# A transformer block with 64 routed experts on one core: the last block of queries split in two, its last tile's rows stored apart, and the jobs put in another order

## The chip, the core and the metric

The kernel runs on one core of a Trainium2 chip, in one launch. The metric is the device time of one execution in microseconds (us). The core has five engines that run on their own instruction streams and wait for each other on semaphores: PE (matrix multiply, with its weight loads listed as PEld), DVE (vector), ACT (activation), POOL (GpSimd) and SP, which here only issues DMAs. DMAs that move whole tiles are issued from SP's queue; those that scatter rows by an index held in a tile are issued from POOL's.

## The reference: what is computed

Two sequences of 512 tokens, 256 features, 16 heads of 16; then 64 experts with inner width 96, 8 of them for each token. All is f32.

```python
x = _layernorm(x + attention(x))            # causal, with a bias per head that grows with the key's position
logits = x @ gate_w.T                       # 1024 tokens, 64 experts
probs = softmax(logits)
topk_w, topk_idx = top_k(probs, 8)          # weights made to sum to 1
g = einsum('th,ehi->tei', x, w1)
u = einsum('th,ehi->tei', x, w3)
y = einsum('te,tei,eih->th', combine_w, silu(g) * u, w2)
x = _layernorm(x + y)
```

The kernel computes each expert only for the tokens that chose it.

## The kernel before

Tokens are handled in 8 tiles of 128 (four per sequence). The attention goes through four blocks of two query tiles each, `blocks_ = [(0, 0), (0, 1), (1, 1), (1, 0)]` (sequence, half): a "short" block has the first two tiles of a sequence, and so one part of keys, a "long" block the last two and two parts. A block takes 8 steps, one for each pair of heads. In one step of the loop written out by hand (it fixes the order on PE, DVE and ACT), PE makes scores for pair `step` (`scores`, line 318; DVE takes maxima, line 324), and for pair `step - 3` the exponentials (`exponentials`: PE line 369, ACT line 379, and POOL cuts the triangle off with an affine select, line 384). Every second step, `values` multiplies with the values (line 406) and copies the result to `raw` (line 415).

When a block's last `values` is done, seven jobs are put into the following steps by `at`: `normalize`, `turn_context`, `project`, `norm` with `turn_x1`, `route`, `weigh` and `find_places`. Together they finish the attention's output, its layer norm, and the routing of two tiles: `find_places` counts with matmuls how many earlier tokens chose each expert (`seen` holds the counts so far) and gets for each token and choice a row number `to` (line 580). Then `dispatch` issues 8 scatters a tile on POOL's queue (line 587): each sends 128 rows of `x1` (the token, its weights, its places) into the DRAM buffer `xg`. There every expert has 288 rows: 128 first places, 32 more, and two further half blocks of 64. All of them are filled at the start with blank rows by 13 DMAs from SP (lines 194 and 195), 23,770 KB in all. POOL's stream keeps affine selects and scatters in a fixed order (`in_order`).

After the attention, a list stage on DVE (lines 697 to 787) works out from the counts which half blocks beyond the first 160 places are used. It needs two small index tiles from POOL (`number`, line 714, and `quarter`, line 752). Then comes a fallback loop (line 899) with a trip count read from the tile `extra` by every engine: it would treat all experts in full if the half blocks did not suffice. For these inputs its count is zero, but all engines meet there.

The expert stage has 88 jobs: 64 "one" (an expert's first 128 places), 16 "four" (the next 32 places of four experts together), 8 "pair" (two half blocks, found at run time). A job is fetched from `xg` by SP (line 793), turned by PE (line 799) and copied by DVE (line 801), multiplied (lines 810, 825, 834), and its 128 result rows are scattered into `results` in DRAM on POOL's queue (line 849). Jobs are fetched eight ahead in program order, and run through four steps, one after the other. A fetch waits for all 64 scatters (`after_scatters`). The weights of the first 18 experts are loaded at the start (`first_places`), 20 more into `room` during the attention (`load_then`), 8 more into `lates` behind it (these three go by pairs of experts), and the last 18 into `first_places` again as those come free. At the end, `results` is loaded back (line 995), eight rows a token are summed with `x1`, and the second layer norm goes out (lines 990 and 991).

## Time and profile before

| what | us |
|---|---|
| median of 9 runs (lowest and highest) | 463.23 (460.69 to 469.13) |
| the profiled execution: its time | 463.45 |
| the profiled execution: its span | 461.8 |
| span up to the last copy of `raw` (line 415) | about 205.6 |
| from there to the first scatter of the last block | about 26.3 |
| from that scatter to the first copy of a job's rows (line 801) | 28.2 |
| first to last scatter of results (line 849) | 266.8 to 426.3 |
| loading `results`, sums, second layer norm | about 33 |

The span runs from the first to the last instruction on the core; the time of the same execution is 1.65 us longer. Busy times: PE 360.1 us (78%), DVE 233.8, POOL 200.9, ACT 162.4. PE's busy time is modelled and overlaps itself, so it is not a bound by itself; the profile's row of the granted PE clock (10 tenths is full speed) tells how fast PE was allowed to go. "Idle before" an instruction is put down to the engine whose signal ended it.

### The profile page before, as it was taken

Reading aid. Unit: us, or ns where it says so; the run is one execution under the profiler, and the core shown is the slowest. Engines: PE = TensorE matmul, PEld = TensorE weight load, DVE = VectorE, ACT = ScalarE, POOL = GpSimd, SP = SyncE. Lnnn points to the kernel's source line nnn. Section 1 sums busy time; section 2 is a strip of 40 time slices with the busy share of each in tenths; the row PEclk is TensorE's granted clock in tenths of the full one; section 3 lists DMA queues with packets and bytes.
Section 4 is the critical chain, followed back from the end, with each engine's and each line's share of the span. In section 5 each row is a group of like instructions: output and inputs, shape, how many; then the busy total and the mean of one; then the engine's idle time right before and its main releaser. Section 6 shows DMA issues by size and latency. Waiting matters only on the chain. (4 is left out here: it accounts for less than half of the span.)

```text
span 461.8 us, 8458 instructions
## 1 busy us (share of the span) xinstructions
PE 360.1 (78%) x2546; PEld 237.2 (51%) x2546; DVE 233.8 (51%) x1040; ACT 162.4 (35%) x453; POOL 200.9 (43%) x278
## 2 busy tenths in 40 slices
PE   4499999998998899685300497898998898997493
PEld 2135545655664566453300365566665666765372
DVE  0744356764865256241390355455555565653185
ACT  2012423464446224424110144343434444435032
POOL 8911221211355337647477055354555455656000
PEclk9799999997999559656555599899999899999598
DMA  8999999999921202324833589997787757211793
GB/s 258 390 340 312 281 300 301 307 293 290 395 99 58 83 29 90 110 73 152 304 116 132 147 235 333 297 298 223 212 252 224 209 152 219 69 68 57 307 411 112
DMA packets 56591, 98.58 MB, mean 213 GB/s; under 512 B 7241, under 2 KB 40600, under 8 KB 55520
## 3 DMA queue, kind: packets, MB, share of 16 engines
q1 hardware_dynamic: 47728, 76.93, 53.8%
q0 software_dynamic: 7456, 19.46, 11.7%
q10 hardware_dynamic: 1360, 1.64, 1.1%
q8 instruction: 21, 0.34, 0.3%
q14 instruction: 26, 0.21, 0.1%
HBM read 52.38 MB, written 48.75 MB: 219 GB/s over the span
## 5 line engine op out<-in xcount | busy, mean ns | idle before, releaser
L849 POOL DMA_INDIRECT results<-y,rows x88 | 86.6, 984 | 87.6 <-DVE xT L801 27.6
L324 DVE CUSTOM_DVE_ANT_0 neg<-ps,mask 128x256 f32<-128x256 f32 (+3 forms) x128 | 57.5, 488 | 43.4 <-PE ps L318 37.1
L587 POOL DMA_INDIRECT xg<-x,to x64 | 63.5, 992 | 22.3 <-issue 16.7
L384 POOL TENSOR_SCALAR_AFFINE_SELECT pr<-pr 128x256 f32<-128x256 f32 x64 | 25.0, 408 | 109.8 <-ACT pr L379 109.8
L379 ACT ACTIVATE pr<-pt 128x384 f32<-128x384 f32 (+1 forms) x96 | 45.4, 523 | 48.4 <-PE pt L369 34.6
L799 PE MATMUL pxT<-ident,xb 128*128 128x128 f32 x176 | 36.4, 289 | 29.7 <-SPq L941 29.2
L801 DVE COPY xT<-pxT 128x256 f32<-128x256 f32 x88 | 37.2, 422 | 36.5 <-DMA xb<-xg 17.3
L799 PEld LDWEIGHTS pxT<-ident,xb 128*128 128x128 f32 x176 | 23.1, 145 | 47.4 <-issue 39.4
L818 ACT ACTIVATE s<-pg 128x96 f32<-128x96 f32 x88 | 22.2, 252 | 65.2 <-PE pg L810 29.4
L842 ACT COPY y<-py 128x256 f32<-128x256 f32 x88 | 32.9, 374 | 21.2 <-PE pxT L799 4.6
L810 PE MATMUL pg<-w,xT 128*32 128x192 f32 (+1 forms) x288 | 40.2, 348 | 0.2 <-DVE xT L801 0.2
L825 PE MATMUL paT<-ident,a 128*96 128x128 f32 x88 | 26.1, 297 | 14.5 <-DVE a L820 6.8
L369 PE MATMUL pt<-ql,kT 32*128 32x256 f32 (+1 forms) x192 | 33.5, 433 | 1.0 <-ACT pr L379 0.9
L273 PE MATMUL pq<-room 128*128 128x512 f32 x64 | 34.2, 671 | 0.0
L318 PE MATMUL ps<-room 32*128 32x128 f32 (+3 forms) x128 | 26.7, 492 | 6.4 <-DVE room L279 6.4
L318 PE MATMUL ps<-kT,qT 32*128 32x384 f32 (+3 forms) x128 | 31.5, 535 | 0.3 <-issue 0.2
L878 DVE CAST rows<-row 128x1 int32<-128x1 f32 x88 | 13.5, 154 | 34.0 <-DMA results<-y,rows 27.7
L810 PEld LDWEIGHTS pg<-w,xT 128*32 128x32 f32 (+1 forms) x288 | 27.9, 156 | 3.1 <-issue 0.8
L834 PE MATMUL py<-w,aT 96*32 96x256 f32 (+1 forms) x144 | 28.5, 390 | 0.0
L369 PE MATMUL pt<-ql,room 32*128 32x256 f32 (+1 forms) x192 | 27.0, 381 | 0.6 <-ACT pr L379 0.6
L827 ACT COPY aT<-paT 96x128 f32<-96x128 f32 x88 | 22.9, 260 | 12.2 <-PE paT L825 8.7
L369 PEld LDWEIGHTS pt<-ql,kT 32*128 32x128 f32 x192 | 22.9, 223 | 7.1 <-ACT pr L379 3.1
(200 smaller groups left out, 617.0 us busy)
## 6 DMA issues: line engine op xcount, KB each, us to landing
xg<-blank SPq DMA_DIRECT2D x8, 2632.0 KB
w<-in_wall_dram SPq DMA_DIRECT2D x18, 640.0 KB
xb<-xg SPq DMA_DIRECT2D x64, 164.5 KB
room<-in_wall_dram SPq DMA_DIRECT2D x10, 640.0 KB
room<-results SPq DMA_DIRECT2D x6, 1024.0 KB
wo<-in_wall_dram SPq DMA_DIRECT2D x16, 320.0 KB
xg<-blank SPq DMA_DIRECT2D x4, 658.0 KB
xb<-xg SPq DMA_DIRECT2D x64, 41.1 KB
```

Of the source, the lines that this page charges most:

```text
L273: nc.tensor.matmul(pq, lhsT=wqk_s[:, t, c, g * P : (g + 1) * P], rhs=xTs_[b][:, c, :], start=(c == 0), stop=(c == DC - 1))
L318: nc.tensor.matmul(ps[:, :n], lhsT=qT[b][r, g, q * P : (q + 1) * P], rhs=kT[b][r, g, :n], start=True, stop=True)
L324: nc.vector.tensor_tensor_reduce(out=junk[:, :n], in0=ps[:, :n], in1=mask[:, S - n :], scale=-1.0, scalar=BIG, op0=ALU.add, op1=ALU.min, a ...
L369: nc.tensor.matmul(pts[n][:, col : col + W2 - first], lhsT=kT[b][r, g, k * P : (k + 1) * P], rhs=ql[r, first:], start=True, stop=True,)
L379: nc.scalar.activation(pr[:, :cols], pts[n][:, :cols], AF.Exp, scale=SCALE)
L587: sc = nc.gpsimd.indirect_dma_start(out=xg[:, :], out_offset=bass.IndirectOffsetOnAxis(ap=tos[s][:, a, k : k + 1], axis=0), in_=x1[:, i + ...
L799: nc.tensor.transpose(pt[:, c * P : (c + 1) * P], xb[:, c * P : (c + 1) * P], ident)
L801: nc.vector.tensor_copy(xT, pt)
L810: nc.tensor.matmul(pg[r * m : (r + 1) * m, :], lhsT=xT[:, c * P + r * m : c * P + (r + 1) * m], rhs=w[:, c * 2 * I : (c + 1) * 2 * I], sta ...
L834: nc.tensor.matmul(py[r * m : (r + 1) * m, :], lhsT=aT[:I, r * m : (r + 1) * m], rhs=w[:I, DC * 2 * I :], start=True, stop=True,)
L842: nc.scalar.copy(y, py)
L849: a = nc.gpsimd.indirect_dma_start(out=results[:, :], out_offset=bass.IndirectOffsetOnAxis(ap=rows, axis=0), in_=y, in_offset=None, bounds ...
```

## The change

It has five parts.

- **Order and units of the attention.** Blocks become `(sequence, first tile, number of tiles)`; the second sequence's short block goes third, its long one last. The jobs behind a block now run per "unit": three units of two tiles, and the last block as two units of one tile each, both in the same steps. The jobs can stand in the middle of a step too, by a table of half steps for each block, and scatters are spread by a second table.
- **The last tile's rows apart.** For the very last unit, `find_places` takes the larger of the count so far and 128 as its base, so that its rows never fall among an expert's first 128 places. `seen` is then the count of used places, holes among them, and the separate count by a matmul goes.
- **Fetches that wait for less.** A "one" job waits for the first 56 scatters only; "four" and "pair" wait for all 64.
- **Order of the jobs.** Twenty "one" jobs go first, then each "four" with 2 or 3 "one" jobs, and a "pair" at every second "four". The late weights are asked for behind "four" jobs.
- **The fallback loop** moves from ahead of the jobs to behind them. The zeros that the loop wrote into `results` are now written always, by eight DMAs from SP of 1024 KB each during attention steps 16 to 23; before, these DMAs stood in the loop and never ran.

```diff
+    def no_results(i):
+        nc.sync.dma_start(
+            results[i * P * TOPK : (i + 1) * P * TOPK, :].rearrange("(p k) d -> p k d", k=TOPK),
+            blank[:, :D].unsqueeze(1).to_broadcast([P, TOPK, D]),
+        )
...
-        blocks_ = [(0, 0), (0, 1), (1, 1), (1, 0)]
+        blocks_ = [(0, 0, 2), (0, 2, 2), (1, 0, 2), (1, 2, 2)]
+        units = [(s, 0, 2) for s in range(len(blocks_) - 1)] + [(len(blocks_) - 1, a, 1) for a in range(2)]
...
+            else:
+                pm = room_for(s, 3)
+                nc.tensor.matmul(pm[:, 0, :], lhsT=ones, rhs=seen, start=True, stop=True)
+                nc.tensor.matmul(pm[:, 1, :], lhsT=before, rhs=mk[:, 0, :], start=True, stop=True)
+                nc.tensor.matmul(pm[:, 2, :], lhsT=ones, rhs=mk[:, 0, :], start=True, stop=True)
+                nc.vector.tensor_scalar(seen, pm[:, 0, :], float(P), None, ALU.max)
+                nc.vector.tensor_tensor(mine, pm[:, 1:2, :], seen.unsqueeze(1), ALU.add)
+                nc.vector.tensor_tensor(seen, pm[:, 2, :], seen, ALU.add)
...
-                scatters.append(sc)
+                if s == len(units) - 1:
+                    tc.add_to_no_dep_group("last scatters", sc.ins)
+                    last_scatters.append(sc)
+                else:
+                    scatters.append(sc)
                 in_order(sc, many=True)
...
+        HALF_STEPS = [[0, 1, 2, 4, 5, 6], [0, 2, 4, 7, 10, 12], [0, 1, 2, 4, 5, 6], [0, 2, 4, 6, 8, 10]]
+        SCATTER = [lambda k: k // 2, lambda k: k // 2, lambda k: k // 2, lambda k: 0]
...
+            for m in range(NT):
+                at(16 + m, no_results, m)
...
+                        for w in mine:
+                            nt = units[w][2]
+                            todo_ = [
+                                [(normalize, w, a) for a in range(nt)],
+                                [(turn_context, w)],
+                                [(project, w)],
+                                [(norm, w), (turn_x1, w)],
+                                [(route, w)],
+                                [(find_places, w), (weigh, w)],
+                            ]
+                            when = HALF_STEPS[s]
+                            for h, job in zip(when, todo_):
+                                for f, *args in job:
+                                    at(step + 1 + h // 2, f, *args, mid=h % 2 == 0)
+                            m = step + 1 + when[-1] // 2
+                            for k in range(0, nt * TOPK):
+                                at(m + SCATTER[s](k), dispatch, w, k, k + 1)
...
-    def after_scatters(ins):
-        for s in scatters:
+    def after_scatters(ins, own_block):
+        if own_block:
+            tc.declare_no_dep(ins.ins, group="last scatters", reason="their rows are in other blocks")
+        for s in scatters if own_block else scatters + last_scatters:
...
-        pc = ps_e.tile([P, E], F32, tag="y", name="pcount")
-        nc.tensor.matmul(pc, lhsT=ones, rhs=seen, start=True, stop=True)
         count = lists.tile([P, E], F32, name="count")
-        nc.vector.tensor_copy(count, pc)
+        nc.vector.tensor_copy(count, seen)
...
-        more = nc.values_load(extra[0:1, 0:1], min_val=0, max_val=E)
-        zeros = lists.tile([P, D], F32, name="zeros")
-        nc.gpsimd.memset(zeros, 0.0)
-        with tc.For_i(0, more, 1) as e:
...
-        jobs = []
+        AT_FIRST = 20
+        jobs = [("one", e) for e in range(AT_FIRST)]
         for j in range(E // 4):
             jobs.append(("four", j))
-            jobs += [("one", e) for e in range(4 * j, 4 * j + 2)]
+            first, end = [AT_FIRST + (E - AT_FIRST) * m // (E // 4) for m in (j, j + 1)]
+            jobs += [("one", e) for e in range(first, end)]
             if j % 2 == 0:
-                jobs.append(("pair", j // 2))
-            jobs += [("one", e) for e in range(4 * j + 2, 4 * j + 4)]
+                jobs.insert(len(jobs) - 1, ("pair", j // 2))
...
-                    kind, e = jobs[n]
-                    pair = NOW + THEN + LATE + e // 2
-                    if kind == "one" and e % 2 and pair < E // 2:
-                        load_weights(pair, first_places[e // 2])
+                    kind, j = jobs[n]
+                    for pair in (2 * j, 2 * j + 1):
+                        if kind == "four" and NOW + THEN + LATE + pair < E // 2:
+                            load_weights(NOW + THEN + LATE + pair, first_places[pair])
+
+        more = nc.values_load(extra[0:1, 0:1], min_val=0, max_val=E)
+        with tc.For_i(0, more, 1) as e:
...
```

The built program shows the order that results on each engine where no hand wrote it. On POOL's stream the two index tiles `number` and `quarter`, which stood ahead of the last block's 16 scatters, now stand behind all 16 scatters of the last two units. On DVE's stream the list stage still stands ahead of the first job's copy, and 14 of its instructions, from the first that reads `number`, stand between that point and the copy. On SP's stream the first 18 fetches of "one" jobs stand in a row.

## The prediction

> **What bounds the kernel now.** I read the slices first, then the chain of waits, the timeline around the seam between attention and jobs, and windows of the job stage.
>
> ```profile
> PE   4499999998998899685300497898998898997493
> POOL 8911221211355337647477055354555455656000
> PEclk9799999997999559656555599899999899999598
> DMA  8999999999921202324833589997787757211793
> ```
>
> A slice is 11.5 us. PE is busy nearly throughout, but for a hole around slices 20 to 22, where POOL works. From slice 13 on to 22 its granted clock is about half.
>
> ```profile
> 230.97 0.17 DVE L580 SCALAR_TENSOR_TENSOR to<-x,beyond 128x16 int32<-128x16 f32 x1
> 231.10 0.14 POOL L714 IOTA number<- 128x8 f32 x1 [5.03 <-DVE x L578]
> 231.90 1.00 POOL L587 DMA_INDIRECT xg<-x,to  x1 [0.30 <-DVE blocks L704]
> ...
> 252.15 0.96 POOL L587 DMA_INDIRECT xg<-x,to  x1 [0.30 <-issue]
> ...
> 256.20 4.90 SPq L793 DMA_DIRECT2D xb<-xg  x8
> ...
> 260.13 0.42 DVE L801 COPY xT<-pxT 128x256 f32<-128x256 f32 x1 [17.25 <-DMA xb<-xg]
> ```
>
> ```profile
> 252.15 2.40 DMA xg<-x,to
> 254.55 0.70 SPq L899
> ```
>
> In the timeline and in the chain the hole has its parts: the last rows' addresses are ready at 231.14; 16 scatters go one behind the other on POOL, from 231.90 to 253.11 (21.2 us, 1.3 each); the last lands at 254.55; SP passes the loop and fetches at 256.20, 1.65 us behind the landing; the first job's copy is at 260.13, 28.2 us behind the first scatter. The list stage on DVE lies beside the scatters.
>
> ```profile
> 148.00:171.00 23.00, 19.77 (x127) 13.82 (x129) 7.37 (x41) 7.61 (x19) 8.19 (x12) 0.50 0.14 49
> 231.00:259.40 28.40, 0.00 (x0) 0.00 (x0) 11.47 (x52) 2.77 (x3) 17.14 (x19) 0.50 0.31 109
> 266.00:300.00 34.00, 29.06 (x219) 20.70 (x219) 17.16 (x92) 13.45 (x51) 16.19 (x17) 0.95 0.91 289
> 388.00:416.00 28.00, 26.45 (x212) 18.70 (x213) 17.81 (x94) 12.78 (x52) 15.75 (x16) 1.00 0.30 96
> ```
>
> Windows: length, busy times of PE, PEld, DVE, ACT and POOL, then clock, DMA share, GB/s. Jobs are counted by POOL's scatters of results: 17 begin from 266 to 300 us (2.00 us each, DMA share 0.91), 16 from 388 to 416 (1.72 from spacing of their starts, share 0.30). Undisturbed, 87 steps would take 149.6 us; first to last scatter took 159.6 (266.76 to 426.35). So 10 us of the job stage is what transfers cost.
>
> **The change, step by step**, against the profiled span of 461.8 us.
>
> *Attention up to the last `raw` copy (205.6 before).* The block order moves PE's work without removing any. What the half steps can remove are places where `values` wait for the routing's exponentials, since both use one PSUM tile:
>
> ```profile
> PE halves L406 <- ACT lg L527: 4.0, 2, 2.1
> DVE nth L566 <- remote: 4.8, 1, 4.8
> ```
>
> Two waits, 4.0 us together; routing now falls on steps without `values`: −4.0. Against it, the first scatter moves from step 19 to step 15, and still waits for the blank rows. SP keeps eight DMAs in flight, and its eighth load behind the last blank DMA was issued by 114.07 (103.50 + 10.57); bandwidth rises from 299 to 378 GB/s at 112 us. So the blanks land near 112. POOL reaches that scatter at about 101.7 (the affine pair of that step ran from 100.88 to 101.67). It waits 10.3 us; two scatters (2.6) and the next affine pair (0.8), ready at 104 before, end at 115.4 instead of 104.97. Who waits are `values`, and those ran at 112.2 before anyhow, held by routing: 3.2 us late, of which the lighter short block behind it can make up some (its steps took 3.22 us on POOL in the old place). I count 0; bounds 0 and 10.4. In the long block POOL now has 23 scatters and 8 affine pairs, 23 × 1.28 + 8 × 0.95 = 37 us, over 8 steps that took 124.9 to 171.4 = 46.5 us: covered; if those steps fell under 4.6 us, POOL would set them.
>
> The zero fill adds eight issues on SP, past which four `room` loads and the next `x1` store are moved; those loads' experts come after 18 jobs, and the store has no reader, so 0. If the fill's transfers held the scatters, landings would grow from 2.40 us to the 6.64 of the chain's slowest results scatter; with eight outstanding at 1.28 us, POOL waits only beyond 10.2 us. So 0, and 2 as a bound from the `remote` row, where a stream stood still during saturated DMA. [...]
>
> Half clock: between 148 and 171 us PE ran at 0.50 while busy 19.77 us. If fewer gaps let it run full, that saves 9.9; if the early wait spreads half clock, it costs as much elsewhere. I count 0. [...]
>
> Attention: −4, bounds −14 and +10.
>
> *From `raw` to the first scatter.* Before: 205.1 to 231.9, 26.8 us. The first scatter now needs only one tile's chain, while the second tile runs between. From the timeline's rows of that stretch, at the same half clock: the context's copy starts behind two transposes instead of four (207.72 for 208.67) and takes 0.37 for 0.58: −1.2; sum 0.42 for 0.69 and one pair of statistics (0.61) fewer ahead: −0.9; norm activation 0.55 for 1.09, transposes 0.70 for 1.40, copy 0.37 for 0.58: −1.4; gate matmuls of one tile (of 1.97 for two) −1.0, but the other tile's transposes stand ahead, +0.7; one top-8 of two (0.48 each) −0.5; two place matmul pairs behind the mask, about 1.0, for 2.40 (222.46 to 224.85): −1.4; place arithmetic 1.9 for 2.4: −0.5; weighing, formerly beside PE, now ahead of the scatter, +1.3 (222.64 to 223.96); index tiles and memset gone from POOL's path, 231.10 to 231.90, −0.6. Sum −5.5. The `remote` wait held DVE 4.8 us, 4.0 beyond PE's end at 224.85, in the time of the 2.5 MB `lates` load; the load is still there, so half of it is taken: −2.0 (bounds 0, −4). Together −7.5.
>
> *From first scatter to first copy.* "One" fetches wait for 8 fewer scatters, which looks like −10.6 us (half of 21.2). But `number` and `quarter` stand on POOL behind all 16 scatters, and DVE's list stage ahead of the first copy. So: 16 scatters 21.2, two index tiles 0.3, the 14 list instructions up to the copy 6.4 (their durations before, less overlap) = 27.9, against 28.2: −0.3. What was saved on the fetch now waits on DVE.
>
> *Jobs.* Same 88, same PE work. The first twenty have their rows and weights in place and no weight load beside them; before, the first 17 cost 17 × 0.28 = 4.8 us above the undisturbed rate. The nine weight loads then fall behind jobs 20 to 36, beside denser "four" jobs, where part is paid again. I take −3; bounds −9 (nearly all 10 gone) and +3 (as much again as I take).
>
> *End.* The loop's meeting now stands between the last result's landing and the load of `results`: 1.65 us there, where SP now goes on 0.2 after landing (428.73, 428.92): +1.5, with 0.1 for the deleted count's matmul and copies set against the extra DVE work: +1.6. The loop's body stays unrun: counting the routing for these inputs, 8 half blocks are needed before and after.
>
> Sum: −4.0 − 7.5 − 0.3 − 3.0 + 1.6 = −13.2. The span becomes 448.6; the profiled execution's time, 463.45, is 0.22 above the median, so the median becomes 463.2 − 13.2 = **450.0 us**.
>
> **Rivals.**
>
> *The fetch decides, not the index tiles.* If DVE's order did not hold the copy, it would come 10.6 (8 scatters) + 2.4 landing + 0.6 issue + 2.4 fetch + 0.7 transposes = 16.7 us behind the first scatter: 11.2 less, 438.8. For it: neither fetch nor PE waits for the last 8 scatters. Against: DVE runs in order.
>
> *The half clock goes.* 450.0 − 9.9 = 440.1. For: fewer waits in the second batch. Against: the short block now runs in the dense part, and clock followed no busy share I could find.
>
> *Nothing left.* The attention ends some 9 us later than forecast, and the seam gives it back: 460 to 463. The part that counts is done but eaten.
>
> *Slower: POOL waiting for the blanks.* The affine pair is 10.4 us late and all of it reaches the last `raw`, while routing, moved ahead, saves nothing: 450.0 + 4.0 + 10.4 = 464.4; with half clock over one more stretch of 23 us, up to 474. It decides the sign when the last `raw` copy comes later than 205.6 + 9.2 = 214.8. For: POOL's stream is in order, and no other engine does the affine. Against: PE was held at that place before too.
>
> **How the numbers follow.** Forecast 0.55 (own range 443 to 457), early fetch 0.10, full clock 0.13, nothing left 0.07, slower 0.15. Faster by over 0.5% (below 460.9; about what a measurement of this kernel can tell) 0.78, within 0.5% 0.07, slower 0.15. The range 438 to 462 reaches the two fast rivals and, above, half of the bounds of attention and jobs; it leaves out the worst of POOL's wait.
>
> **What would show it.** The last `raw` copy at 199 to 205 us; first scatter of the second-last tile near 220; `number` on POOL right behind the 16th scatter, and the first copy 27 to 28 us behind the first scatter, with PE's transposes done some 10 us before; first twenty jobs at 1.7 us or less; about 1.6 us between last landing and the load of `results`. Wrong if POOL's first scatter is long over at 112, if the copy comes before the last scatter, or if the attention's end moves by more than 10 us.

## The result and the profile after

| what | before | after | change |
|---|---|---|---|
| median (runs) | 462.88 (31) | 473.71 (10) | ratio 1.0204, interval 1.017 to 1.0238 |
| profiled span | 461.8 | 470.1 | +8.3 |
| span up to the start of the last copy of `raw` | 205.2 | 219.6 | +14.3 |
| from there to the first of the last 16 scatters | 26.7 | 16.5 | -10.2 |
| from that scatter to the first copy of a job's rows | 28.2 | 25.8 | -2.4 |
| from that copy to the first scatter of results | 6.6 | 7.1 | +0.5 |
| first to last scatter of results (88 jobs) | 159.6 | 165.5 | +5.9 |
| from there to the end | 35.5 | 35.5 | +0.1 |

The changed kernel is slower by 2.0%; 450.0 us (438 to 462) had been forecast. Executions of one kernel differ by 2% and more (459.66 to 469.13 us for the kernel before, 468.54 to 482.81 for the changed one), and groups of runs by 4% (medians of the kernel before from 443.1 to 462.6), so ratios below are always to the kernel before as timed in the same group of runs, and two profiles are compared with care. A ratio is taken over the executions in the faster of the two states in which this kernel runs, so it can differ from the ratio of two medians of all executions. The changed kernel, run once more in another group (e9), came out at 1.0074 (1.0015 to 1.0133): it is slower in both groups, but by how much isn't steady.

The page's slices after (PE, POOL, granted PE clock, DMA; a slice is 11.75 us):

```profile
PE   4399999879878898986501689888798889897494
POOL 8901222103871153476476055554544555556000
PEclk9799999998996587677655699998989999999599
DMA  8999999999999621122478475798778766311793
```

The hole between attention and jobs is again at slices 20 and 21, of a longer span. POOL now has a block of work in slices 10 and 11, the first scatters; DMA is full until slice 13, where the zero fill ends; and the clock is low in the same half of the attention as before, in other slices.

The timeline at the seam, after:

```profile
236.07 0.97 POOL L626 DMA_INDIRECT xg<-x,to  x1 [6.74 <-issue]
...
248.13 23.94 SPq L847 DMA_DIRECT2D xb<-xg  x24
...
250.66 1.45 PE L853 MATMUL pxT<-ident,xb 128*128 128x128 f32 x4 [16.08 <-DMA xb<-xg]
...
255.23 0.97 POOL L626 DMA_INDIRECT xg<-x,to  x1 [0.31 <-issue]
256.21 0.16 POOL L768 IOTA number<- 128x8 f32 x1
...
256.41 0.23 DVE L769 TENSOR_SCALAR number<-number,half 128x8 f32<-128x8 f32 x1 [11.33 <-issue]
...
261.90 0.42 DVE L855 COPY xT<-pxT 128x256 f32<-128x256 f32 x1
```

The fetch goes out 7.1 us ahead of the 16th scatter's issue, and PE has turned the first rows by 252.1. But `number` is made by POOL behind all 16 scatters, DVE stands still for 11.33 us until then, and the copy comes 9.8 us after PE was done with its rows.

What PE waited for, from 80 to 222 us, after (total, times, longest):

```profile
PE px1T L512 <- ACT x L500: 5.1, 4, 1.8
PE pt L384 <- issue: 3.9, 2, 3.5
...
PE halves L422 <- ACT lg L555: 1.7, 1, 1.7
PE halves L592 <- ACT lg L555: 1.5, 2, 1.3
PE halves L422 <- DVE v L301: 1.5, 1, 1.5
```

Of the 4.0 us before in which `values` waited for the routing's exponentials 1.7 are left, as forecast in kind; but the place matmuls now wait for them (1.5), and others are new.

Windows after (length, busy PE, PEld, DVE, ACT, POOL, clock, DMA share, GB/s): the third block, the fourth, and three stretches of the jobs.

```profile
126.00:167.00 41.00, 33.45 (x230) 21.58 (x234) 22.87 (x104) 14.46 (x32) 17.34 (x28) 0.72 0.88 309
167.00:219.50 52.50, 44.17 (x337) 27.62 (x329) 18.89 (x74) 21.58 (x45) 26.84 (x39) 0.73 0.21 74
```

```profile
269.00:303.00 34.00, 29.89 (x189) 25.08 (x187) 19.96 (x101) 14.56 (x57) 18.77 (x20) 0.95 0.67 191
303.00:350.00 47.00, 40.01 (x307) 25.75 (x304) 22.63 (x123) 17.42 (x65) 21.55 (x22) 0.93 0.82 259
400.00:430.00 30.00, 27.44 (x232) 18.55 (x232) 17.30 (x94) 12.19 (x48) 16.61 (x17) 1.00 0.19 64
```

The first twenty jobs went at 1.70 us each with the DMA share down to 0.67 (it was 0.91), as forecast. Scatters 20 to 40 then took 43.3 us where the kernel before took 36.5.

**Where the attention's 14 us went.** Windows of half a microsecond over the attention show a pattern. From the changed kernel:

```profile
139.50:140.00 0.50, 0.00 (x0) 0.00 (x0) 0.47 (x5) 0.49 (x2) 0.00 (x0) 1.00 0.98 326
...
140.50:141.00 0.50, 0.00 (x0) 0.00 (x0) 0.00 (x0) 0.50 (x3) 0.50 (x2) 0.98 0.93 316
141.00:141.50 0.50, 0.43 (x1) 0.18 (x1) 0.00 (x0) 0.50 (x2) 0.00 (x1) 0.50 1.03 342
...
147.00:147.50 0.50, 0.50 (x8) 0.39 (x3) 0.00 (x0) 0.00 (x0) 0.03 (x1) 0.50 0.92 340
147.50:148.00 0.50, 0.50 (x7) 0.14 (x2) 0.00 (x0) 0.00 (x0) 0.00 (x0) 0.69 0.89 340
148.00:148.50 0.50, 0.50 (x11) 0.43 (x6) 0.44 (x1) 0.00 (x0) 0.00 (x0) 1.00 0.98 338
```

PE stands still for 1.64 us (waiting for ACT's layer norm), the clock falls to 0.50 at 141.0, and it stays there until 147.8 although PE is busy almost without a break: 6.8 us. In the kernel before a gap of 2.30 us, up to 105.7, is followed by half clock from 107.2 to 114.0, 6.8 us again.

Read in windows of 0.1 us, the two profiles have these stretches of half clock in the attention, here with PE's idle time (a window's length less PE's busy time) in the 3.41 us ahead of each (half the length of the shortest of them, 6.83):

| kernel | half clock, us | length | PE idle in the 3.41 us ahead |
|---|---|---|---|
| before | 107.2 to 114.0 | 6.8 | 2.13 |
| before | 148.1 to 172.0 | 23.9 | 0.87 |
| before | 189.1 to 213.0, past the last copy of `raw` | 23.9 | 1.53 |
| after | 103.4 to 110.3 | 6.8 | 1.30 |
| after | 141.0 to 147.8 | 6.8 | 2.15 |
| after | 151.2 to 168.3 | 17.1 | 0.45 |
| after | 181.9 to 195.6 | 13.7 | 1.45 |
| after | 202.4 to 209.3 | 6.8 | 1.97 |
| after | 212.7 to 219.5 | 6.8 | 1.78 |

Windows around the first fall of each, from the kernel before and then from the changed one:

```profile
103.80:107.20 3.40, 1.32 (x12) 0.94 (x14) 1.19 (x6) 2.19 (x5) 0.79 (x2) 0.99 0.99 233
107.20:110.60 3.40, 3.40 (x22) 2.55 (x20) 1.31 (x6) 1.26 (x3) 0.00 (x0) 0.50 0.95 234
110.60:114.00 3.40, 3.40 (x32) 1.67 (x32) 2.27 (x11) 1.57 (x6) 0.79 (x2) 0.50 1.00 354
```

```profile
93.16:96.57 3.41, 2.56 (x42) 1.42 (x30) 1.42 (x6) 1.78 (x4) 0.79 (x2) 1.00 1.08 288
96.57:99.99 3.42, 2.33 (x20) 1.62 (x21) 0.57 (x3) 1.87 (x4) 0.00 (x0) 1.00 1.07 318
99.99:103.40 3.41, 2.11 (x22) 1.60 (x21) 3.06 (x16) 1.83 (x8) 0.79 (x2) 1.00 1.07 261
103.40:106.81 3.41, 3.41 (x21) 2.63 (x20) 1.61 (x7) 0.52 (x2) 0.00 (x0) 0.51 0.99 253
```

In the changed kernel a stop of 1.77 us, from 95.7 to 97.5, left the clock at 1.00: the first two windows have 0.85 and 1.09 us of idle PE. The third, with a stop of 1.30 us up to 103.0, was followed by a fall. So most falls follow stops of PE, seven of these nine 1.30 us or more of idle time, but not all: those at 148.1 and 151.2 follow 0.87 and 0.45 us. And 1.48 us of idle PE from 89.8 to 93.2 in the changed kernel were followed by none. What brings the clock down is not shown by this.

The attention's length splits into three parts. With b the busy time of PE in a window of half a microsecond and c its clock, work is the sum of b times c, lost to the clock the sum of b times (1 - c), idle the rest. From the first affine select (38.84 before, 39.26 after) to the last copy of `raw`:

| | length | work | PE idle | lost to the clock | falls of the clock |
|---|---|---|---|---|---|
| before | 166.4 | 131.5 | 15.3 | 19.7 | 3 |
| after | 180.3 | 132.4 | 22.1 | 26.1 | 6 |

The work is nearly the same. The change added 6.8 us in which PE stood still and 6.4 us lost to half clock: it has six falls of the clock in place of three.

The chain that ended last, at the point where the fallback loop now stands:

```profile
434.56 2.32 DMA results<-y,rows
436.88 0.02 SPq L1011
...
437.71 0.33 SPq L1043
```

The last results land at 436.88, SP passes the loop (line 1011) in 0.83 us and loads them.

### The profile page after: what moved, and what is told of

Same layout as the page of the kernel before. It is cut to its first block, busy times and chain, and to the rows that moved or that the text cites. A ratio compares the mean times of both kernels' runs of the same rounds, so it can differ in the third digit from the quotient of the medians.

```text
span 470.1 us, 8491 instructions
## 1 busy us (share of the span) xinstructions
PE 367.2 (78%) x2544; PEld 239.1 (51%) x2544; DVE 236.6 (50%) x1056; ACT 162.7 (35%) x456; POOL 199.8 (43%) x277
## 3 DMA queue, kind: packets, MB, share of 16 engines
q10 hardware_dynamic: 1360, 1.64, 1.0%
## 5 line engine op out<-in xcount | busy, mean ns | idle before, releaser
L334 DVE CUSTOM_DVE_ANT_0 neg<-ps,mask 128x256 f32<-128x256 f32 (+3 forms) x128 | 57.2, 487 | 50.5 <-PE ps L328 30.1
L626 POOL DMA_INDIRECT xg<-x,to x64 | 62.5, 977 | 35.3 <-issue 22.9
L853 PE MATMUL pxT<-ident,xb 128*128 128x128 f32 x176 | 37.1, 294 | 16.2 <-DMA xb<-xg 16.1
L879 PE MATMUL paT<-ident,a 128*96 128x128 f32 x88 | 26.6, 302 | 19.3 <-DVE a L874 16.2
L853 PEld LDWEIGHTS pxT<-ident,xb 128*128 128x128 f32 x176 | 23.9, 148 | 33.0 <-issue 25.7
L328 PE MATMUL ps<-kT,qT 32*128 32x128 f32 (+3 forms) x128 | 33.2, 616 | 1.6 <-DVE maxima L334 1.3
L879 PEld LDWEIGHTS paT<-ident,a 128*96 128x96 f32 x88 | 11.2, 127 | 34.5 <-DVE a L874 24.3
L888 PE MATMUL py<-w,aT 96*128 96x256 f32 (+1 forms) x144 | 28.6, 391 | 0.0
L881 ACT COPY aT<-paT 96x128 f32<-96x128 f32 x88 | 22.8, 260 | 13.2 <-PE paT L879 10.6
L384 PE MATMUL pt<-ql,room 32*128 32x256 f32 (+1 forms) x192 | 26.0, 376 | 0.5 <-issue 0.3
```

The costliest lines, as they stand in the source:

```text
L328: nc.tensor.matmul(ps[:, :n], lhsT=qT[b][r, g, q * P : (q + 1) * P], rhs=kT[b][r, g, :n], start=True, stop=True)
L334: nc.vector.tensor_tensor_reduce(out=junk[:, :n], in0=ps[:, :n], in1=mask[:, S - n :], scale=-1.0, scalar=BIG, op0=ALU.add, op1=ALU.min, a ...
L384: nc.tensor.matmul(pts[n][:, col : col + nt * P - first], lhsT=kT[b][r, g, k * P : (k + 1) * P], rhs=ql[r, first : nt * P], start=True, st ...
L626: sc = nc.gpsimd.indirect_dma_start(out=xg[:, :], out_offset=bass.IndirectOffsetOnAxis(ap=tos[s][:, a, k : k + 1], axis=0), in_=x1[:, i + ...
L853: nc.tensor.transpose(pt[:, c * P : (c + 1) * P], xb[:, c * P : (c + 1) * P], ident)
L879: nc.tensor.transpose(pa[:I, :], a, ident)
```

## The experiments

Eighteen runs were made, in five groups; each group timed the kernel before beside its own (462.6, 445.0, 444.6, 458.7 and 443.1 us; their chips are numbered 5, 7, 10, 7 and 8). All but e13 and e18, which start from the kernel before, are the changed kernel with the edits named. "Attention" below is the length just defined.

**e1, the index tiles made at the start.**

```diff
+    number = const.tile([P, NPS], F32, name="number")
+    nc.gpsimd.iota(number, pattern=[[2, NPS]], base=0, channel_multiplier=0, allow_small_or_imprecise_dtypes=True)
...
     begin = const.tile([P, E], F32, name="begin")
...
-        number = lists.tile([P, NPS], F32, name="number")
-        nc.gpsimd.iota(number, pattern=[[2, NPS]], base=0, channel_multiplier=0, allow_small_or_imprecise_dtypes=True)
```

and the same for `quarter`.

> The changed kernel with the two index tiles (number, quarter) made by POOL at the start instead of in the list stage; the same computation. In the changed kernel the first job's rows are turned at 252.1 us, but the copy of them starts at 261.9, behind list instructions on DVE that waited for these two tiles, which POOL made at 256.2 behind its 16th scatter. If the index tiles hold the copy (the step of the prediction), it comes at 252.3 to 253.5 here, 16 to 17.5 us behind the first of the last scatters, and the time falls by 8 to 10 us, to 464 (ratio 1.003). Rival: the next thing holds it or the jobs after it (the last eight scatters, which 'four' jobs wait for, or the DMAs): the copy comes early, but the first twenty jobs stretch, and less than 4 us are left at the last result scatter (470 or more, ratio over 1.012).

465.27 us (the median of all twelve executions), ratio 0.9995 (0.9959 to 1.003), against 1.0204 for the changed kernel and 1.0191 for e3 in its own group. The timeline of e1:

```profile
242.32 0.97 POOL L630 DMA_INDIRECT xg<-x,to  x1 [6.58 <-issue]
...
257.21 0.66 PE L853 MATMUL pxT<-ident,xb 128*128 128x128 f32 x2 [16.40 <-DMA xb<-xg]
257.91 0.43 DVE L855 COPY xT<-pxT 128x256 f32<-128x256 f32 x1 [3.81 <-issue]
```

The copy follows PE at once, 15.6 us behind the first scatter in place of 25.8, and the ratio falls by 2%. The index tiles held the copy, as the prediction had it. Of these 10.2 us, 7.5 are left at the first scatter of results (267.76, 25.4 us behind the first scatter of rows in place of 33.0), and the jobs behind it took no longer (163.1 us, 165.5 in the changed kernel).

**e2, e3, e4: one part of the attention's change at a time.** e2 leaves the zero fill out; e3 shifts the third block's scatters three steps (`3 + k // 2`); e4 has the old steps (and weighs ahead of the places, as the kernel before did):

```diff
-        HALF_STEPS = [[0, 1, 2, 4, 5, 6], [0, 2, 4, 7, 10, 12], [0, 1, 2, 4, 5, 6], [0, 2, 4, 6, 8, 10]]
-        SCATTER = [lambda k: k // 2, lambda k: k // 2, lambda k: k // 2, lambda k: 0]
+        HALF_STEPS = [[1, 5, 7, 9, 11, 13]] * 3 + [[0, 2, 4, 6, 8, 10]]
+        SCATTER = [lambda k: 1 + k // 2, lambda k: 1 + k // 2, lambda k: 1 + k // 4, lambda k: 0]
```

> The changed kernel without the eight DMAs that write zeros into results (for these inputs every row of results is written by a job and the fallback loop does not run, so the output is unchanged). If the fill's 8.4 MB hold up other transfers in the attention, the stretch from 113 to 157 us, where DMA is at 0.9 to 1.0, relaxes and the last copy of raw comes 3 to 5 us earlier than at 219.6 (time 469, ratio 1.010). If the fill lies beside everything, as the prediction's term of 0 (bound 2) has it, the last copy of raw stays at 218 to 220 and the time at 472 to 474 (ratio 1.017 to 1.022).

> The changed kernel with the third block's 16 scatters three steps later, so that no step holds two scatters of each of two units. In the changed kernel the last three steps of the long last block hold four scatters each (5.1 us) and an affine pair (0.9), and took about 7 us each. If POOL's stream bounds those steps, they fall to about 5.5 and the last copy of raw comes 4 to 5 us earlier, at 215 (time 469; less where the late scatters meet the last units' own). If PE, DVE and ACT bound them, the last copy of raw stays within 1.5 us of 219.6, and the later scatters push the last units' first one back by up to 5 us (time 474 to 478).

> The changed kernel with the jobs behind the first three blocks put back to one a step at the step's end, weighing ahead of the places, and scatters from the step after, as in the kernel before; block order, last block in two units, fill, jobs and loop as changed (the third block's scatters four a step, so that they end ahead of the last units'). If the half steps cost what the attention lost, the last copy of raw comes at 206 to 210 in place of 219.6, and the time falls by 8 to 12 us, to 463 (ratio 1.000). If the block order or the fill cost it, the last copy of raw stays at 217 or later and the time at 471 or more (ratio over 1.014). If it is half of each: 212 to 215, ratio 1.008.

e2: one execution took 467.6 us and five 477.3 to 485.4, which gives no usable interval; no gain is shown. e3: 1.0191 (1.0143 to 1.024): the attention fell by 3 us to 177.2, and the last units' first scatter came 22.7 us behind it in place of 16.5. PE idled 15.8 us in place of 22.1, so POOL's crowded steps were a cause of stops, but the clock took 4.0 of these 6.3 us back (table below). e4: 1.0313 (1.0262 to 1.0364), attention 178.3. All three miss their first theory, and only with the split into idle and clock (table below) does e4 become readable: its PE idles 16.2 us, as little as before, with three falls of the clock, but those last 27.3, 20.5 and, up to the last copy of `raw`, 25.3 us.

**e5, e6: the old order of blocks, and the whole old attention.**

```diff
-        blocks_ = [(0, 0, 2), (0, 2, 2), (1, 0, 2), (1, 2, 2)]
+        blocks_ = [(0, 0, 2), (0, 2, 2), (1, 2, 2), (1, 0, 2)]
```

That is e5; e6 has e4's steps too, weighs first and has no fill.

> The changed kernel with the second batch's long two tiles third and its short two last (the short ones now as the two units of one tile, the last one's rows apart), as the order was before; half steps, scatter tables, fill, jobs and loop as changed. Counted from the first affine pair of the attention, the last copy of raw came after 166.4 us in the kernel before and after 180.3 in the changed one. If the order of the two blocks is what the attention lost, it comes after 162 to 170 here, and the time falls by 10 to 15 us, to 460 (ratio 0.990 to 0.998). Rival, the fill and POOL's wait for the blanks, which are both still there: it stays after 175 us or later and the ratio over 1.012.

> The changed kernel with the attention of the kernel before: long block third, one job a step at the step's end, weighing first, no zero fill (its rows are all written by jobs here); only the last block stays in two units of one tile, with the last tile's rows apart; jobs and loop as changed. If the half steps were worth what the prediction took for them (4 us), this is 4 us slower than the last run with the long block third, and the last copy of raw comes 166 us behind the first affine pair. If the half steps cost time, or the fill does, it is faster than that run. By the terms measured in the changed kernel (last raw to first scatter -10.2, to first result -1.9, jobs +5.9) the time is 463 - 6 = 457 (ratio 0.987).

e5: 1.0203 (1.0145 to 1.026), attention 176.3: a miss, the order alone is not it. e6: 0.9965 (0.993 to 1.0001), attention 161.1. With the old attention the loss is gone; what is left of the change is worth 0 to 0.7%, less than the 1.3% expected, since e6's first scatter (224.31) stood behind scatters of the third block on POOL, though its addresses and weights were ready at 219.0.

**e9 to e12: order, half steps and fill one by one.** e9 is the changed kernel again; e10 is e6 with the fill; e11 has the half steps and their table of scatters alone, e12 the new order alone.

> The changed kernel itself, run beside the next three, since chips differ: one call's kernel before took 462.6 us, another's 445.0, and the difference lay in the jobs (first to last scatter of results 159.6 and, in the fast call's kernels, about 148). By the first measurement the ratio is 1.0204; on a faster chip the attention's loss weighs more, up to 1.03.

> The kernel of e6 (order and steps of before, last block in two units) with the zero fill. In e6 the last copy of raw came 161.1 us behind the first affine pair; with half steps and fill together (e5) 176.3. If the fill alone costs it, it comes after 170 us or later here and the ratio is 1.010 or more. If the fill lies beside the rest, it comes after 160 to 166 and the ratio stays at 0.995 to 1.000.

> Order of before and the half steps, without the fill. If the half steps cost what e5 lost against e6, the last copy of raw comes 174 to 178 us behind the first affine pair and the ratio is 1.015 to 1.022. If the fill cost it, 160 to 166 and 0.995 to 1.000. If they cost only together, the same as without the half steps.

> Short block third and long one last, with one job a step as before and without the fill. If the order of the blocks costs by itself, the last copy of raw comes 175 us or later behind the first affine pair and the ratio is above 1.020. If order costs only with the half steps or the fill beside it, 161 to 168 and 0.995 to 1.003.

The ratios are in the table below; each of the three parts alone has a worse one than e6. PE's waits in the attention of e11 and then of e6, which differ in the half steps, in the table of scatters and in whether weighing or the places come first:

```profile
PE halves L422 <- POOL pr L399: 6.6, 2, 4.3
PE px1T L512 <- ACT x L500: 4.0, 2, 2.2
...
PE halves L422 <- ACT lg L555: 1.3, 1, 1.3
```

```profile
PE px1T L512 <- ACT x L500: 6.0, 4, 2.3
PE halves L422 <- ACT lg L555: 4.7, 3, 2.3
```

The half steps take 3.4 us of waits for the exponentials away, as the prediction had it, and 2.0 for the layer norm. In their place `values` waits 6.6 us for the affine pairs: in steps 31 to 33 POOL has two scatters of each of two units, four at 1.28 us, ahead of the next pair.

**e14, the first scatters later.** `SCATTER[0]` becomes `4 + k // 2`, steps 19 to 26 as before.

> The changed kernel with the first block's scatters four steps later, at steps 19 to 26, where the kernel before had them; everything else as changed. In the changed kernel's profiles the first scatter waited for the blank rows 5.75, 8.70, 9.57 and 0.84 us, and the last copy of raw came 180.3, 182.3, 182.4 and 172.4 us behind the first affine pair. If this wait, through the affine pair behind it, sets what the attention loses, the last copy of raw comes after 168 to 173 us here on any chip, and the ratio is 0.997 to 1.005. If POOL's crowded last steps and the rest of the schedule set it, it stays at 178 or later where the changed kernel's would, and the ratio is 1.010 or more.

POOL's first scatter in the profiles of e8 (the changed attention), of the changed kernel, and of e14, one fence each:

```profile
118.14 1.05 POOL L626 DMA_INDIRECT xg<-x,to  x1 [9.57 <-DMA room<-in_wall_dram]
```

```profile
114.33 1.05 POOL L626 DMA_INDIRECT xg<-x,to  x1 [5.75 <-DMA room<-in_wall_dram]
```

```profile
125.69 1.05 POOL L626 DMA_INDIRECT xg<-x,to  x1 [0.70 <-DMA results<-blank]
```

In the first two the trace names a load of `room`, issued behind the blank rows, as what ended the wait; that the blank rows held it is inferred. In e14 it is down to 0.70 us, and the attention is still 178.4 us, ratio 1.0153 (1.0096 to 1.021). PE idled 5.6 us less than in the changed kernel and lost 5.2 us more to the clock. The rival that had POOL waiting for the blanks gave about the right time, 464 to 474 us, by luck: it is not the cause, or not the main one.

All runs of the attention in one table, worked out as above (idle and clock in us; a last stretch of half clock is counted up to the last copy of `raw`):

| kernel | order, steps, fill | attention | PE idle | lost to the clock | falls | ratio |
|---|---|---|---|---|---|---|
| before; e13; e18 | old, old, no | 166.4; 161.6; 160.7 | 15.3; 15.6; 14.7 | 19.7; 14.9; 16.6 | 3; 3; 3 | |
| e6 | old, old, no | 161.1 | 15.3 | 16.3 | 3 | 0.9965 |
| e15; e16; e17 | as e6 | 165.8; 161.5; 161.2 | 15.3; 15.2; 15.3 | 21.2; 16.0; 16.1 | 3; 3; 3 | other parts differ |
| e10 | old, old, yes | 167.6 | 16.5 | 22.7 | 3 | 1.0100 (1.0054 to 1.0145) |
| e12 | new, old, no | 166.5 | 16.3 | 17.9 | 4 | 1.0196 (1.0087 to 1.0305) |
| e4 | new, old, yes | 178.3 | 16.2 | 31.3 | 3 | 1.0313 |
| e11 | old, half, no | 173.8 | 21.6 | 23.7 | 4 | 1.0169 (1.0071 to 1.0267) |
| e5 | old, half, yes | 176.3 | 22.8 | 24.7 | 5 | 1.0203 |
| changed; e9 | new, half, yes | 180.3; 172.4 | 22.1; 17.8 | 26.1; 24.1 | 6; 6 | 1.0204; 1.0074 |
| e1; e7; e8 | as changed | 183.6; 182.3; 182.4 | 19.1; 22.1; 23.8 | 33.9; 28.6; 27.0 | 9; 6; 6 | other parts differ |
| e3 | new, half, yes, scatters apart | 177.2 | 15.8 | 30.1 | 7 | 1.0191 |
| e14 | new, half, yes, scatters late | 178.4 | 16.5 | 31.3 | 6 | 1.0153 |
| e2 | new, half, no | 187.1 | 21.9 | 34.7 | 9 | - |

Work lies between 128.7 and 132.4 in all. Each kernel with the half steps has four to nine falls of the clock, 15.8 to 23.8 us of idle PE, and at least 23.7 us lost to the clock; with the old steps it is three or four falls, 14.7 to 16.5 us idle and, but for e4, at most 22.7 lost. A row shows one execution, while the ratio comes from several: e12's profiled execution took 443.7 us, the fastest of six with a median of 449.8, and e2's was the slowest of its six. Any one of the three parts, put alone on the old attention, makes the ratio worse by 0.013 to 0.023 against e6 (another group). They don't add: e4 with old steps is the slowest of all by its ratio, and e9, with all three, is no slower than e10, e11 or e12 in their own group. How much the order and the fill cost by themselves isn't settled, for the clock alone moves the same attention by 5 us (before, e13); that the half steps with their table of scatters made PE stop more often and longer is shown by e11 against e6 and by e5 against e10. e3 and e14 keep the half steps and move one block's scatters alone, and PE idles 15.8 and 16.5 us, about as with the old steps: so most of the added idle time hangs on where POOL's scatters stand, while the falls of the clock, 7 and 6, stay.

**e7, e13, e16: the order of the jobs.** e7 is the changed kernel with the old job order; e13 the kernel before, profiled beside e14; e16 is e15 (below) with the old job order.

> The changed kernel with the jobs in the order before, the late weights asked for behind the 'one' jobs as before. From first to last scatter of results the 88 jobs took 159.6 us before and 165.5 in the changed kernel. If the new order costs that, they take 160 here and the time falls to 468 (ratio 1.010; the first job is a 'four' again and waits for all 64 scatters, which gives back up to 2 us of it). If the stretch came from elsewhere (the clock, the scatters' landing), they still take 164 or more and the ratio is 1.018 or more.

> The kernel before, profiled on the chip of these runs. On the first chip its 88 jobs took 159.6 us from first to last scatter of results and the changed kernel's 165.5; on faster chips the new order took 146 to 148 and (e7) the old one 152. If the new order of jobs costs time everywhere, the old one takes 3 us or more less than the new one here too; if what it costs hangs on the chip's transfers, the old one takes as long or longer here when the chip is a fast one.

> The same with the jobs and the late weights in the order before. Its first job is a 'four', which needs all 64 scatters, so the first copy of a job's rows comes some 10 us later than in the run beside it. If the new order is worth only that, this ratio is 0.020 above the other; if the new order costs time in the jobs, the jobs here take 3 to 6 us less from first to last scatter of results and the ratio is only 0.010 above.

Times from the first scatter of results to number 20, from there to 40, and to the last, in us, new order against old in the same group:

| | first 20 | next 20 | the rest | all |
|---|---|---|---|---|
| changed against before | 36.7, 39.9 | 43.3, 36.5 | 85.5, 83.2 | 165.5, 159.6 |
| e14 against e13 | 34.9, 38.1 | 42.3, 36.0 | 84.4, 81.5 | 161.6, 155.6 |
| e5 against e7 | 31.1, 37.9 | 39.3, 37.8 | 77.3, 76.7 | 147.7, 152.4 |
| e15 against e16 | 35.4, 40.8 | 35.8, 34.7 | 88.4, 85.4 | 159.5, 161.0 |

The first twenty gain 3 to 7 us and the rest pays back 2 to 9. So the new order's cost in the jobs changes its sign: 6 us in the first two pairs, a gain of 1.5 to 5 in the others (e5 and e7 differ in their attention too). That it only moves the weights' transfers fits these rows, but isn't shown. e7's ratio was 1.0296 (1.0243 to 1.0349), and e16 gave 0.9974 (0.993 to 1.0017) where e15 gave 0.983.

**e8, e18: more buffers for row numbers**, on the changed kernel and on the kernel before. The tile of results, `y`, gets more too, 14 in e8 and 12 in e18 for 10; no run takes the two apart.

```diff
-            ri = work.tile([P, 1], I32, tag="rows", name=f"rows{n}", bufs=6)
+            ri = work.tile([P, 1], I32, tag="rows", name=f"rows{n}", bufs=14)
```

> The changed kernel with 14 buffers in place of 6 for the jobs' row numbers (tile rows) and 14 in place of 10 for their results (tile y). DVE waited 15.3 us in the changed kernel, and 27.7 in the kernel before, to write row numbers while the scatter that read the buffer six jobs earlier had not landed. If these waits set the rate of the jobs, first to last scatter of results falls from 165.5 us to 153 to 158 and the time to 464 (ratio 1.003 or less). If the DMA engines' own load or PE sets it, the wait moves to another place and the jobs still take 163 us or more (ratio 1.015 or more).

> The kernel before with 14 buffers for row numbers (6 before) and 12 for results (10); nothing else changed. DVE waited 27.7 us in its jobs for scatters six jobs back. If these waits set the rate, its 88 jobs fall from 155.6 to 159.6 us (two chips) to 150 or less and the ratio is 0.975 to 0.985. If the transfers set it, the wait moves elsewhere and the ratio is 0.993 or more.

What DVE waited for in the jobs, e5 (6 buffers) and e8 (14) in the same group:

```profile
DVE rows L932 <- DMA results<-y,rows: 28.4, 29, 2.7
DVE xT L855 <- PE pxT L853: 14.6, 46, 0.9
```

```profile
DVE xT L855 <- PE pxT L853: 23.3, 83, 0.6
DVE a L874 <- ACT s L872: 8.2, 25, 1.2
```

The wait for scatters six jobs back is gone, and the 88 jobs take 140.5 us in place of 147.7. e8's ratio is 0.9989 (0.9954 to 1.0025), e18's 0.9846 (0.9789 to 0.9903): a gain by itself, on the kernel before too, that no part of the change had touched.

**e15, e17: what is left when the parts that lose are taken out.** e15 is e6 with e1's index tiles and e8's buffers. e17 also asks for the late weights behind the first jobs:

```diff
-        for m in range(LATE):
-            load_weights(
...
                 if step + AHEAD < total:
                     fetch(step + AHEAD)
+                if step % 2 == 0 and 4 <= step < 4 + 2 * LATE:
+                    m = step // 2 - 2
+                    load_weights(
...
```

> The kernel of e6 (attention in the order and steps of before without the fill; last block in two units, rows apart, fetches that wait for less, new order of jobs) with the index tiles made at the start (e1) and 14 buffers for row numbers and results (e8). If the gains add, e6's ratio of 0.9965 falls by 0.018 to 0.021 for the index tiles and by 0.015 to 0.020 for the buffers: 0.955 to 0.965. If the early jobs only run into the weights' load or the last eight scatters, 0.975 to 0.985.

> The kernel of e15 with the four loads of late weights (2.5 MB) asked for behind the first jobs instead of ahead of the first fetch. In e15 the first job's rows were turned at 241.5 us but their copy came at 258.4: DVE's list stage, 5.5 to 8 us of work, was cut into pieces by six waits of about 2 us that no semaphore explains (remote, issue), and one of 7.8, with the DMA engines at a share of 0.7 to 0.8. If the late loads starve DVE there, the copy comes 16 to 18 us behind the first of the last scatters here (32 in e15) and the ratio is 0.960 to 0.970 in all runs. If the fetches themselves or the scatters do it, the copy still comes 25 us or more behind and the ratio stays at 0.983 to 0.995.

e15: ratio 0.983 (0.9737 to 0.9923). DVE's waits in e15 from the first of the last scatters to the first jobs, in a longer execution of 460.3 us span, and then in e17 (424.8 us, another chip); `remote` and `issue` mean that the profile names no releaser:

```profile
DVE seen L609 <- remote: 7.8, 1, 7.8
DVE blocks L760 <- issue: 2.4, 1, 2.4
DVE den L583 <- remote: 1.9, 1, 1.9
DVE over L759 <- remote: 1.9, 1, 1.9
DVE upto L762 <- remote: 1.9, 1, 1.9
```

```profile
DVE xT L853 <- PE pxT L851: 8.5, 1, 8.5
```

In e15 DVE's list stage was stopped again and again where no semaphore of the trace explains it, and the first copy came 32.4 us behind the first scatter. In e17 it ran through, waited for PE alone, and the copy came 15.9 us behind. e17's ratio is 0.964 (0.9569 to 0.971): faster than both kernels. That the late loads cause the stops fits the pair, but e15 and e17 ran on different chips. Of the kernels with these loads in the old place, the kernel before, e4, e13 and e16 had one such stop of 4.8 to 7.6 us, and e1, e6 and e9 had none; so the cause isn't shown.

## Why the prediction was wrong, point by point

- **Attention, -4.0 forecast, +14.3 measured: the step that failed.** The prediction summed two waits on `halves` and took them off; they shrank from 4.0 to 1.7 us, but PE's stops grew by 6.8 us in all. It did not ask what else was put into the steps the jobs moved to: place matmuls that wait for the exponentials (1.5), `values` for `v` (1.5) and, in e11, for POOL (6.6), and in the changed kernel one stop of 3.5 us in the last steps, beside POOL's crowded queue, which the trace puts to no engine. POOL was looked at ("37 us ... covered") as a sum over the block, not by steps. A list of one line's waits is not a list of PE's stops.
- **Half clock, counted 0 with bounds of 9.9: mis-sized.** "Clock followed no busy share I could find", and so new stops of PE were not counted for what the clock might add to them; in the two profiles seven of nine falls follow 1.30 us or more of idle PE within 3.41 us. The slices that the prediction read as half clock "from slice 13 on to 22" hold one at 9 tenths, and so two separate falls, at 148.1 and at 189.1 us. Half clock cost 6.4 us more here than in the kernel before, and 10 to 12 us more in e3, e4 and e14. Four of the changed kernel's six stretches lasted 6.8 us, three of them with PE busy nearly throughout the first half (0.00, 0.09 and 0.20 us idle in 3.41).
- **POOL waiting for the blanks**: counted 0, and the slower rival built on it. The wait came (0.8 to 9.6 us), but e14, all but without it, is nearly as slow.
- **Zero fill, 0 with a bound of 2**: e10 against e6 is worse by 0.0135, with 6.4 us more lost to the clock. But in e10 the clock had fallen at 105, ahead of the fill's first DMA at 107.3, and stayed down for 17 us, where e6's fell at 110 and stayed down for 10. Not settled.
- **`raw` to first scatter, -7.5 forecast, -10.2 measured: right for the units, too small for the `remote` wait.** In e18, the old units without the `remote` wait, this took 21.5 us; the changed kernel took 16.5. So the two units are worth -5.0 (forecast -5.5), and -5.2 is the wait that was not there in this execution (forecast -2.0 with a bound of -4; it is 6.6 us in e13 and none in e18, both with the old units, so this part is luck and not the change's doing).
- **First scatter to first copy, -0.3 forecast, -2.4 measured: right.** DVE waited behind the index tiles; the scatters took 20.1 us (21.2 forecast) and the list instructions 5.5 (6.4). The rival with an early fetch put the copy at 16.7 us without that wait; e1 measured 15.6.
- **Jobs, -3 forecast, +5.9 measured: the second failed step.** The first twenty did what was forecast (-3.2); "part is paid again" was more than all of it: "four" jobs took 2.54 us each on average in place of 2.25, beside the weights' loads. In other groups the same order gained (the table of jobs), so the size of this term stays open.
- **End, +1.6 forecast, +0.1 measured.** The loop's meeting took 0.83 us, not 1.65, between landing (436.88) and the load (437.71), where 0.19 lay before; the rest of the end was 0.5 shorter.

Ahead of the terms stands the range: the attention's bounds of -14 and +10 came from single rows, and the loss of 14.3 lay above the upper one, so that 473.7 fell outside 438 to 462.

## What to carry to other kernels

Before work is spread into the gaps of a dense stream on PE, list every stop of PE of a microsecond or more, not the waits of one line. Count each new one at its own length and about as much again for the clock (an estimate from the two profiles above, where 6.8 us more of idle PE came with 6.4 us more lost to half clock). Where an early fetch is made possible, follow every queue up to the first use: two index tiles of 0.16 us behind 16 scatters held the first copy for 10 us here, and six small buffers for row numbers, with ten for results, held the jobs by 7. And split a stretch into work, idle and clock before comparing two profiles of it: the same kernel's attention differed by 5 us in the clock alone.

## What the runs showed of the hardware

- The granted clock of PE went between 1.00 and 0.50 in the attention: in the kernel before it was 0.50 three times, for 6.8, 23.9 and 23.9 us (the last of them past the last copy of `raw`), in the changed kernel six times, for 6.8 to 17.1 us. Other runs had stretches as short as 3.4 us (e9, 104.3 to 107.7) and as long as 27.3 (e4, 103.5 to 130.8). In the changed kernel a stop of 1.30 us (up to 103.0) was followed by half clock for 6.8 us, while one of 1.77 us (up to 97.5) was not.
- Groups of runs differ in the jobs more than in the attention: the same order of jobs took 165.5, 161.6 and 146.1 us (changed, e14, e9), while work in the attention stayed within 3%. Whether the chip makes this difference isn't known: e5 and e14, on chips of the same number, took 147.7 and 161.6.
